# Recurrent matmuls of an LSTM split by gate, and two convolution chunks moved into the projection

## The chip, the core and the metric

The kernel runs on one core of a Trainium2 chip. The metric is the device time of one execution in microseconds (us). Three runs of the kernel before took 1895.57, 1897.46 and 1898.66 us; the median is 1897.46 us. About 0.2% (3.8 us) is what such a measurement can tell from no change.

## What is computed

Two layers, each added to its input. `x` has 8 sequences of 512 steps and 512 features, `cond` one vector of 512 features for each sequence.

```python
# layer 0: LSTM over the 512 steps, h0 = cond, c0 = 0
a = x_t @ Wx + b + h @ Wh              # 8 x 2048: gates i, f, o, g, 512 columns each
c = sigmoid(f) * c + sigmoid(i) * tanh(g)
h = sigmoid(o) * tanh(c)
x = x + h                              # for every step
# layer 1: convolution, projections, scan
# (cond is taken as the 8 taps, one for each of 8 steps)
conv = cb + sum(x_pad[:, k:k + L] * cond[k] for k in range(8))
proj = conv @ Wp + bp                  # 512 -> 128
B_t, C_t = softplus(proj[..., :64]), tanh(proj[..., 64:])
u = x @ Ws + bs
state = decay * state + dt * B_t * u;  y = C_t * state
x = x + y @ Wo + bo
```

## The kernel before

The LSTM is a chain of 512 steps, each of which needs the h of the one before. All instructions of the loop are issued in an order written out by hand; each engine works through its own queue in that order and waits on semaphores.

**Matmuls of a step.** h is held as the stationary operand (`stat`, two buffers that alternate by step): four chunks k of 128 rows, 16 columns of float16 (8 sequences, a high and a low part); in odd steps 32 columns are loaded, of which 16 belong to the step. The weights stream as the moving operand, in two float16 parts, high (`whh`) and low (`whl`). The array is used as four column tiles q of 32, so four matmuls with the same k and part form a group that runs side by side and fills 4 x 32 partitions. The gates of the hidden chunks 0 and 1 form half A, those of chunks 2 and 3 half B. Each half has 256 columns of weights: 64 for each of g, i, f and o. `h_mm` (L308) issues 8 matmuls for one half and one k; the order of (half, k) is `PE_ORDER` (L25). Chunks k = 0, 1 of h come from half A of the step before, k = 2, 3 from half B, so the matmuls with k = 2 or 3 can only start when half B is done too. After the 64 matmuls of h come `bias_mm` (L293) and `x_mm` (L299) of a later step: a bias group and eight groups that multiply x with Wx, 36 matmuls of 256 columns. They start the sum of a pair of steps in the PSUM tile `hp`, which has a bank of its own for each half, twice; half A is started in even steps, half B in odd ones.

**The gates of a step.** The class `Chain` (L549) has one method for each operation, and `ORDER` (L23) names them one after the other, the letter first, then the half: `TA` is T of half A. T (L569) transposes the 192 columns of g, i, f from PSUM on VectorE, t (L572) the 64 columns of o; a (L576, VectorE) and b (L581, GpSimd) add the high and the low part; g (L585) and o (L588) are the tanh on ScalarE, with the sigmoids written as tanh and the weights scaled to suit; v (L591) and c (L595) form the new cell state on VectorE; k (L598) is its tanh and p (L601) its copy into the next step's tile, both on ScalarE; i (L604), m (L607) and l (L610) form h, its high part into `stat`, its full value into `hb`, and its low part into `stat`. Operation l of half A releases the next step's first matmul.

**Layer 1 as filler.** Layer 1 is cut into 14 blocks of 32 steps, one more of 32, and ones of 16, 8 and 8. The work of a block is queued in the class `Filler` (L34) once its steps are through, and is popped a little in each step: one float32 matmul behind the x matmuls (`pl`, `pl2`), VectorE operations at `f` in ORDER up to a planned sum of FILL = 0.8 us (`dve`, `d2`, `xd`), two ScalarE operations at `E`. From step 480 on up to three planned units of matmuls are popped in each step. What is left after the last step is drained at the end. A float32 matmul of 128 x 256 shows as two records in the trace. Their outputs go to the tiles `fps` (two banks); a chain of matmuls holds its bank until it has been read.

The convolution of a block can go two ways for each chunk of 128 features. With the chunk in `pk`, its 8 taps are folded into 8 copies of Wp (`wpj`), and 8 matmuls (L497) do convolution and projection at once. Otherwise one ScalarE operation (L485) and seven VectorE operations (L480) form the convolution, and one matmul projects it (L498). pk is the third number of a row of `l1blocks` (L97): before, it is 0 for all blocks of 32 steps and 4, 4, 2 for the last three.

**PSUM.** Eight banks: four for `hp`, two for `zp` (the sums after a), two for `fps`.

Of the kernel before, what the change touches and what calls it, by code (L numbers as in the profile page):

```python
# [9 lines left out]
F32 = mybir.dt.float32  # L10
# [7 lines left out]
BLK = 32  # L18
NT = BLK * NB
EXP1 = float(1 << 23)  # L20
FMAX = 65504.0

ORDER = "TA tA aA gA bA TB vA oA aB gB cA tB kA pA bB oB vB iA mA cB lA kB pB iB mB lB f q E"  # L23

PE_ORDER = ((0, 0), (0, 1), (1, 0), (0, 2), (0, 3), (1, 1), (1, 2), (1, 3))  # L25
DUMMY = 4
FILL = 0.8
TAILD = 14
LN2 = 0.6931471805599453

# [60 lines left out]
def lstm_conv_ssm_kernel(ctx: ExitStack, tc: tile.TileContext, xT, condT, wx, wh, brow, cbp, wpp, bpp,  # L91
                         wsp, bsp, alogp, dtlogp, wop, bop, outT):
    nc = tc.nc
    T = xT.shape[2]
    NBLK = T // BLK

    l1blocks = [(i * BLK, BLK, 0) for i in range(NBLK - 2)]  # L97
    l1blocks += [(T - 64, 32, 0), (T - 32, 16, 4), (T - 16, 8, 4), (T - 8, 8, 2)]
    v, s, pe, sp = nc.vector, nc.scalar, nc.tensor, nc.sync

    cp = ctx.enter_context(tc.tile_pool(name="cp", bufs=1))
    st = ctx.enter_context(tc.tile_pool(name="st", bufs=2))
    pp = ctx.enter_context(tc.tile_pool(name="pp", bufs=1, space=PSUM))
# [3 lines left out]
    wb = [[cp.tile([128, 4, 4, 512], F16, name=f"w{m}{p}") for p in "hl"] for m in "hx"]  # L107
# [26 lines left out]

    seen = cp.tile([128, 1], F32, name="seen")
    v.memset(seen, 0.0)
    s.activation(seen, seen, AF.Tanh)

    seq = [(0, 0), (1, 0), (1, 1), (1, 2), (1, 3), (0, 1), (0, 2), (0, 3)]
# [20 lines left out]
    gate = [[cp.tile([128, 128], F32, name=f"gate{h}{i}") for i in range(4)] for h in range(2)]  # L160
    x2b = [cp.tile([128, 4, 7 * NB + NT], F32, name=f"x2b{i}") for i in range(3)]

    hpb = [[pp.tile([128, 512], F32, name=f"hp{h}{i}") for i in range(2)] for h in range(2)]
    hp = [[t[:, 0:256] for t in r] for r in hpb]

    zp = [pp.tile([128, 64], F32, name=f"zp{i}") for i in range(2)]
    fps = [pp.tile([128, 2 * NT], F32, name=f"fps{i}") for i in range(2)]

    pool = nc.gpsimd
    ident = cp.tile([128, 128], F32, name="ident")  # L170
# [116 lines left out]

    def warm(n, w):
        for _ in range(n):
            pe.matmul(fps[1][:, 0:256], ident, w, start=True, stop=True)  # L290


    def bias_mm(P, h):  # L293

        for q in range(4):
            pe.matmul(hp[h][P % 2][32 * q:32 * q + 32, :], bst[P > 0][:, q], bmov[:, 256 * h:256 * h + 256],  # L296
                      start=True, stop=False, tile_position=(0, 32 * q), skip_group_check=True)

    def x_mm(P, h, ks):  # L299
        S = xs[P // (BLK // 2) % 2]  # L300
        for k in ks:
            for W in wb[1]:
                for q in range(4):
                    pe.matmul(hp[h][P % 2][32 * q:32 * q + 32, :], S[:, k, P % (BLK // 2)],  # L304
                              W[:, k, q, 256 * h:256 * h + 256],
                              start=False, stop=False, tile_position=(0, 32 * q), skip_group_check=True)

    def h_mm(t, h, ks):  # L308
        S = stat[t % 2]
        o = 16 * (t % 2)  # L310
        for k in ks:
            for wi, W in enumerate(wb[0]):
                for q in range(4):
                    pe.matmul(hp[h][(t // 2) % 2][32 * q:32 * q + o + 16, :], S[:, k, 0:o + 16],  # L314
                              W[:, k, q, 256 * h:256 * h + 256],
                              start=False, stop=(k == 3 and wi == 1),
                              tile_position=(0, 32 * q), skip_group_check=True)


    v.tensor_scalar(bmov[0:64], braw, 1.0 / 2048, None, op0=ALU.mult)  # L320
# [77 lines left out]
    lo(7, 1)  # L398
    for j in range(2):
        v.tensor_scalar(CL[:, j], SW[:, :, 0], FMAX * (1 - 2 * j), None, op0=ALU.mult)  # L400
    for h in range(2):
        bias_mm(0, h)
    for c, (m, k) in enumerate(seq):
        for h in range(2):
            x_mm(0, h, (k,)) if m else h_mm(0, h, (k,))

    cv = carve(0, 0, (4, NT))
    e, w, x = (carve(0, 1024 + 256 * i, (NT,), 64) for i in range(3))
# [140 lines left out]
    class Chain:  # L549
# [4 lines left out]
        def __init__(self, t, half):  # L554
            h = half
            self.o = 16 * (t % 2)
            self.S = stat[(t + 1) % 2][:, 2 * h:2 * h + 2, 16 - self.o:32 - self.o]
            self.G, self.Gn = gate[h][t % 4], gate[h][(t + 1) % 4]
            self.P, self.zp = hp[h][(t // 2) % 2], zp[h]
            self.hf = hb[(t // BLK) % 2][:, 2 * h:2 * h + 2, t % BLK, :]  # L560
            self.inv = 1.0 if t else INV0
            self.Z = st.tile([128, 6, 32], F32, tag=f"Z{h}", name=f"Z{t}_{h}")
            self.Zo = st.tile([128, 2, 32], F32, tag=f"Zo{h}", name=f"Zo{t}_{h}", bufs=4)
            self.zo = st.tile([128, 16], F32, tag=f"zo{h}", name=f"zo{t}_{h}", bufs=4)
            self.u = st.tile([128, 2, 16], F32, tag=f"u{h}", name=f"u{t}_{h}")
            self.tc = st.tile([128, 16], F32, tag=f"tc{h}", name=f"tc{t}_{h}", bufs=4)

        def T(self):
            v.transpose(self.Z.rearrange("p g r -> p (g r)"), self.P[:, 0:192])  # L569

        def t(self):
            v.transpose(self.Zo.rearrange("p g r -> p (g r)"), self.P[:, 192:256])  # L572

        def a(self):
            o = self.o
# [35 lines left out]

    def dummy(n):
        for _ in range(n):
            pe.matmul(hpb[0][0][:, 0:256], wb[0][1][:, 0, 0, 0:128], wb[0][0][:, 0, 0, 0:256], start=True, stop=True)

    def r8(a):
        return a.rearrange("p (k b) -> p k b", b=8)
# [2 lines left out]
    for t in range(T):  # L620
        n, r = divmod(t, BLK)
        if r == 0:
            assert all(h["x2"] in fl.done for h, (b0, *_) in zip(hist, l1blocks) if b0 < t - BLK)
            load_x(n + 2)
            if n + 1 < NBLK:
                add_x(n + 1, 0, t)
        if nl1 < len(l1blocks) and l1blocks[nl1][0] + l1blocks[nl1][1] <= t:
            add_l1(nl1, *l1blocks[nl1])
            nl1 += 1
        if t:  # L630
            for h, k in PE_ORDER:
                h_mm(t, h, (k,))

        P = t // 2 + 1
        if 2 * P < T:
            assert P < 6 or all( xlast[2 * P // BLK, k] in fl.done for k in range(4))
            bias_mm(P, t % 2)
            x_mm(P, t % 2, range(4))
        room = (1 if t < T - 32 else 3) if 2 * P < T else 4
        while room > 0:  # L640
            cost = fl.pop("pl2", t) or fl.pop("pl", t)
            room -= cost
            if not cost:
                break
        ch = {"A": Chain(t, 0), "B": Chain(t, 1)}
        for op in ORDER.split():
            if op == "f":
                left = FILL
                while True:
                    got = fl.pop("xd", t, left) or fl.pop("d2", t, left) or fl.pop("dve", t, left)  # L650
                    left -= got
                    if not got:
                        break
            elif op == "q":

                if t % 2:
                    s.activation(seen, ch["B"].tc[:, 0:1], AF.Copy)
            elif op == "E":
                for _ in range(2):
                    fl.pop("xa", t) or fl.pop("al2", t) or fl.pop("al", t)  # L660
                fl.pop("po", t)
            else:
                getattr(ch[op[1]], "o_" if op[0] == "o" else op[0])()
        fl.pop("sp", t)
    dummy(TAILD)
    while nl1 < len(l1blocks):
        add_l1(nl1, *l1blocks[nl1])
# [8 lines left out]
def layout(x, cond, Wx, Wh, b, cb, Wp, bp, Ws, bs, Al, dl, Wo, bo):  # L676


    import numpy as np

    def rows(w):
        w = w.reshape(4, 4, 32, -1)
        return np.ascontiguousarray(w.transpose(0, 2, 1, 3).reshape(128, 4, -1))

    order = [3, 3, 0, 0, 1, 1, 2, 2] * 2
    chunk = [0, 1] * 4 + [2, 3] * 4
    T = x.shape[1]
    gx = rows(Wx).reshape(128, 4, 4, 4, 4, 32)
    gh = rows(Wh).reshape(128, 4, 4, 4, 4, 32)
    gb = b.reshape(4, 4, 4, 32)  # L690
    wx = np.stack([gx[:, :, g, :, k, :] for g, k in zip(order, chunk)], 3).reshape(128, 4, 4, 512)
    wh = np.stack([gh[:, :, g, :, k, :] for g, k in zip(order, chunk)], 3).reshape(128, 4, 4, 512)
    bb = np.zeros((2, 32, 16, 32), np.float32)
    for n, (g, k) in enumerate(zip(order, chunk)):
        bb[:, 4 * (g != 3):4 * (g != 3) + 4, n] = gb[g, :, k, :]
    bb = bb.reshape(64, 512)
    xT = rows(x.transpose(2, 1, 0).reshape(512, T * 8)).reshape(128, 4, T, 8)
    cT = rows(cond.T)
    wo = Wo.reshape(64, 4, 4, 32).transpose(0, 2, 1, 3).reshape(64, 4, 128)
    c1 = lambda a: np.ascontiguousarray(a.reshape(-1, 1))  # L700
    d = dict(xT=xT, condT=cT, wx=wx, wh=wh, brow=bb, cb=rows(cb)[:, :, 0], wp=rows(Wp), bp=c1(bp),
             ws=rows(Ws), bs=c1(bs), alog=c1(Al), dtlog=c1(dl), wo=wo, bo=rows(bo)[:, :, 0])
    return {k: np.ascontiguousarray(a) for k, a in d.items()}
# [30 lines left out]
```

## Time and profile before

| | |
|---|---|
| median of three runs | 1897.46 us |
| profiled execution, its own time | 1898.87 us |
| its span | 1897.1 us |
| first T of step 0 / of step 511 | 40.97 / 1858.47 us |
| behind the first T of step 511 | 38.55 us |
| granted TensorE clock, mean | 0.992 |
| TensorE matmul busy | 1653.8 us (87%) |
| VectorE busy | 1648.8 us (87%) |
| ScalarE / GpSimd busy | 782.2 / 288.2 us |

Read it so: 511 steps lie between the first T of step 0 and that of step 511, 3.557 us each on average. The busy shares are averages over steps that are all alike in the recurrent part and differ in the filler that they hold. A matmul record lasts from its issue to its modelled end, so the records of groups that follow each other overlap: what a group costs is the distance between the starts of two groups.

### The profile page before, as it was taken

Reading aid. Unit: us, or ns where it says so; the run is one execution under the profiler, and the core shown is the slowest. Engines: PE = TensorE matmul, PEld = TensorE weight load, DVE = VectorE, ACT = ScalarE, POOL = GpSimd, SP = SyncE. Lnnn points to the kernel's source line nnn. Section 1 sums busy time; section 2 is a strip of 40 time slices with the busy share of each in tenths; the row PEclk is TensorE's granted clock in tenths of the full one; section 3 lists DMA queues with packets and bytes.
Section 4 is the critical chain, followed back from the end, with each engine's and each line's share of the span. In section 5 each row is a group of like instructions: output and inputs, shape, how many; then the busy total and the mean of one; then the engine's idle time right before and its main releaser. Section 6 shows DMA issues by size and latency. Waiting matters only on the chain.

```text
span 1897.1 us, 119869 instructions
## 1 busy us (share of the span) xinstructions
PE 1653.8 (87%) x51861; PEld 1364.6 (72%) x51861; DVE 1648.8 (87%) x9137; ACT 782.2 (41%) x4684; POOL 288.2 (15%) x1110
## 2 busy tenths in 40 slices
PE   6888898898988889898898988889898898988896
PEld 4777777777777777777777777777776777777786
DVE  8778889898898989889898898989889898898984
ACT  5544344344434444443444434434443344434342
POOL 1211111111111111111111111111111111111110
PEclk9999999999999999999999999999999999999997
DMA  6000000000000000000000000000000000000000
GB/s 237 4 4 15 4 26 4 4 27 4 26 4 4 27 4 26 4 26 4 4 27 4 26 4 5 26 4 27 4 26 4 4 15 4 15 4 15 4 13 15
DMA packets 21428, 33.52 MB, mean 18 GB/s; under 512 B 2592, under 2 KB 19616, under 8 KB 19872
## 3 DMA queue, kind: packets, MB, share of 16 engines
q1 hardware_dynamic: 20656, 25.71, 4.0%
q8 instruction: 405, 6.64, 1.5%
q14 instruction: 127, 1.04, 0.2%
q10 hardware_dynamic: 240, 0.13, 0.0%
HBM read 17.45 MB, written 8.39 MB: 14 GB/s over the span
## 4 chain that ended last, share of the span: by engine, by line
DVE 50%; PE 31%; ACT 11%; POOL 4%; issue 4%; DMA 0%; ACTq 0%; POOLq 0%; DVEq 0%
PE hp L314 20%; DVE Z L569 16%; DVE wraw L480 7%; DVE zp L576 6%; PE hp L304 5%; ACT gate L585 5%; POOL zo L581 4%; DVE stat L610 3%; DVE stat L604 3%; ACT gate L588 3%; PE fps L501 3%; DVE u L591 3%; DVE Zo L572 3%; ACT tc L598 3%; DVE hb L607 2%
## 5 line engine op out<-in xcount | busy, mean ns | idle before, releaser
L314 PE MATMUL hp<-whh,stat 128*16 128x256 f16 (+1 forms) x16384 | 932.8, 274 | 212.8 <-DVE stat L610 208.4
L314 PEld LDWEIGHTS <-stat 128*16 128x16 f16 x32768 | 777.2, 93 | 443.8 <-DVE stat L610 374.2
L314 PE MATMUL hp<-whl,stat 128*16 128x256 f16 (+1 forms) x16384 | 928.9, 273 | 0.2 <-DVE whl L279 0.2
L585 ACT ACTIVATE gate<-zp 128x48 f32<-128x48 f32 x1022 | 216.2, 212 | 906.1 <-DVE zp L576 903.6
L569 DVE STREAM_TRANSPOSE Z<-hp 128x192 f32<-128x192 f32 x1024 | 391.6, 382 | 111.7 <-PE hp L314 98.4
L304 PE MATMUL hp<-wxh,xs 128*32 128x256 f16 x8192 | 481.6, 273 | 5.5 <-DVE xs L354 5.5
L581 POOL TENSOR_TENSOR zo<-Zo 128x16 f32<-128x16 f32 x1024 | 245.1, 239 | 1571.5 <-DVE zp L576 1092.4
L304 PE MATMUL hp<-wxl,xs 128*32 128x256 f16 x8192 | 481.6, 273 | 0.0
L304 PEld LDWEIGHTS <-xs 128*32 128x32 f16 x16384 | 438.9, 97 | 15.4 <-DVE xs L354 5.7
L588 ACT ACTIVATE gate<-zo 128x16 f32<-128x16 f32 x1022 | 220.6, 216 | 158.1 <-POOL zo L581 141.6
L604 DVE SCALAR_TENSOR_TENSOR stat<-gate,tc 128x16 f16<-128x16 f32 x1024 | 179.5, 175 | 69.0 <-ACT tc L598 0.6
L572 DVE STREAM_TRANSPOSE Zo<-hp 128x64 f32<-128x64 f32 x1024 | 229.9, 225 | 0.0
L576 DVE TENSOR_TENSOR zp<-Z 128x48 f32<-128x48 f32 x1024 | 211.2, 206 | 0.0
L610 DVE TENSOR_TENSOR stat<-hb,stat 128x16 f16<-128x16 f32 x1024 | 179.3, 175 | 17.5
L591 DVE SCALAR_TENSOR_TENSOR u<-gate 128x32 f32<-128x32 f32 x1024 | 175.9, 172 | 20.9 <-ACT tc L598 0.2
L480 DVE SCALAR_TENSOR_TENSOR wraw<-x2b,cond,wraw 128x256 f32<-128x256 f32 (+1 forms) x434 | 188.7, 472 | 4.7 <-ACT wraw L483 4.7
L601 ACT ACTIVATE gate<-zp 128x16 f32<-128x16 f32 x1024 | 188.5, 184 | 0.0
L607 DVE SCALAR_TENSOR_TENSOR hb<-gate,tc 128x16 f32<-128x16 f32 x1024 | 186.3, 182 | 0.0
L598 ACT ACTIVATE tc<-zp 128x16 f32<-128x16 f32 x1024 | 185.2, 181 | 0.4 <-DVE zp L595 0.2
L595 DVE SCALAR_TENSOR_TENSOR zp<-u 128x16 f32<-128x16 f32 x1024 | 177.3, 173 | 0.0
L296 PE MATMUL hp<-bmov,bst 128*32 128x256 f16 x2048 | 144.5, 273 | 0.0
L296 PEld LDWEIGHTS <-bst 128*32 128x32 f16 x2048 | 54.7, 97 | 3.2 <-issue 0.3
(121 smaller groups left out, 739.2 us busy)
## 6 DMA issues: line engine op xcount, KB each, us to landing
x<-in_xT_dram SPq DMA_DIRECT2D x15, 512.0 KB, 4.0
out_dram<-wraw SPq DMA_DIRECT2D x15, 512.0 KB, 4.1
wraw<-in_wh_dram SPq DMA_DIRECT2D x4, 1024.0 KB, 13.7
wraw<-in_wx_dram SPq DMA_DIRECT2D x4, 1024.0 KB, 10.9
x<-in_xT_dram SPq DMA_DIRECT2D x2, 256.0 KB, 12.9
wp<-in_wp_dram SPq DMA_DIRECT2D x1, 256.0 KB, 7.1
out_dram<-wraw SPq DMA_DIRECT2D x1, 256.0 KB, 2.8
out_dram<-wraw SPq DMA_DIRECT2D x2, 128.0 KB, 2.2
```

The source lines that it names most:

```text
L304: pe.matmul(hp[h][P % 2][32 * q:32 * q + 32, :], S[:, k, P % (BLK // 2)], W[:, k, q, 256 * h:256 * h + 256], start=False, stop=False, tile ...
L314: pe.matmul(hp[h][(t // 2) % 2][32 * q:32 * q + o + 16, :], S[:, k, 0:o + 16], W[:, k, q, 256 * h:256 * h + 256], start=False, stop=(k == ...
L480: v.scalar_tensor_tensor(cv[:, k, 0:N], src, cond[:, k, j:j + 1], cv[:, k, 0:N], op0=ALU.mult, op1=ALU.add)
L569: v.transpose(self.Z.rearrange("p g r -> p (g r)"), self.P[:, 0:192])
L572: v.transpose(self.Zo.rearrange("p g r -> p (g r)"), self.P[:, 192:256])
L576: v.tensor_tensor(self.zp[:, 0:48].rearrange("p (g b) -> p g b", b=8), self.Z[:, :, o:o + 8], self.Z[:, :, o + 8:o + 16], op=ALU.add)
L581: pool.tensor_tensor(self.zo.rearrange("p (g b) -> p g b", b=8), self.Zo[:, :, o:o + 8], self.Zo[:, :, o + 8:o + 16], op=ALU.add)
L585: s.activation(self.G[:, 0:48], self.zp[:, 0:48], AF.Tanh, scale=self.inv)
L588: s.activation(self.G[:, 48:64], self.zo, AF.Tanh, scale=self.inv)
L598: s.activation(self.tc, self.zp[:, 48:64], AF.Tanh, scale=0.5)
L604: v.scalar_tensor_tensor(self.S[:, :, 0:8], r8(self.G[:, 48:64]), 1.0, r8(self.tc), op0=ALU.add, op1=ALU.mult)
L610: v.tensor_tensor(self.S[:, :, 8:16], self.hf, self.S[:, :, 0:8], op=ALU.subtract)
```

## The change

- **The columns of the weights are put in another order** (`layout`): half A's g, i, f (192 columns, called A), half B's o (64, called b), half B's g, i, f (192, called B), half A's o (64, called a).
- **The h matmuls are issued in two parts.** The first, ahead of the gates, has the groups A and B, 16 groups of four matmuls with 192 columns each. The second, at `H` in ORDER behind TB, has a and b, 16 groups with 64 columns each. So 128 matmuls take the place of 64.
- **The outputs.** A's sums and b's share a bank of `hpb[0]`, B's have `hpb[1]`, and a's have one new bank `hpo`, without a second buffer. One bank of `fps` is given up for it.
- **The x matmuls** stand at `X` in ORDER, behind tB: in even steps a bias group and eight groups of 256 columns (A and b together), in odd steps the same number of 192 (B) and again of 64 (a).
- **ORDER is new**: t of half A comes behind TB, g of half B ahead of o of half A, vB and cB ahead of iA, pA behind mA.
- **r and R** are new small copies, in each step and in each odd step: on VectorE one column of the cell state that ScalarE wrote, on VectorE and GpSimd one column each, in odd steps.
- **PK = 2**: in all blocks of 32 steps the chunks 0 and 1 of the convolution go through `wpj`. For a block that takes 2 ScalarE and 14 VectorE operations of 256 columns away, and puts 16 float32 matmuls in the place of 2.
- The three banks `hpb[0][0]`, `hpb[0][1]` and `hpb[1][1]` are given to the filler's matmuls after the last step.

In the order of the changed program, 367 steps have one filler matmul of TensorE behind them, 24 have two to four, and 121 none; before it was 170, 18 and 324. Two VectorE fillers stand in 268 steps, before in 377. After the last step 78 float32 matmuls are left, before 73.

```diff
-ORDER = "TA tA aA gA bA TB vA oA aB gB cA tB kA pA bB oB vB iA mA cB lA kB pB iB mB lB f q E"
-PE_ORDER = ((0, 0), (0, 1), (1, 0), (0, 2), (0, 3), (1, 1), (1, 2), (1, 3))
+ORDER = "TA r aA gA TB H tA bA aB vA tB X cA gB bB oA vB cB kA iA mA pA oB lA kB iB pB mB lB f q R E"
+PE_ORDER = ("A0h A0l A1h A1l B0h A2h A2l A3h A3l B0l B1h B1l B2h B2l B3h B3l",
+            "a0h a0l a1h a1l a2h a2l a3h a3l b0h b0l b1h b1l b2h b2l b3h b3l")
+COLS = {"A": (0, 192), "b": (192, 256), "B": (256, 448), "a": (448, 512)}
+PK = 2
...
-    l1blocks = [(i * BLK, BLK, 0) for i in range(NBLK - 2)]
-    l1blocks += [(T - 64, 32, 0), (T - 32, 16, 4), (T - 16, 8, 4), (T - 8, 8, 2)]
+    l1blocks = [(i * BLK, BLK, PK) for i in range(NBLK - 2)]
+    l1blocks += [(T - 64, 32, PK), (T - 32, 16, 4), (T - 16, 8, 4), (T - 8, 8, 2)]
...
-    hp = [[t[:, 0:256] for t in r] for r in hpb]
+    hpo = pp.tile([128, 512], F32, name="hpo")
-    fps = [pp.tile([128, 2 * NT], F32, name=f"fps{i}") for i in range(2)]
+    fps = [pp.tile([128, 2 * NT], F32, name="fps0")]
+    def sums(c, P):
+        if c == "a":
+            return hpo[:, 0:64]
+        return hpb[c == "B"][P % 2][:, slice(192, 256) if c == "b" else slice(0, 192)]
...
+    XG = ("Ab", "B", "a")
+    def group(P, g):
+        if g == "Ab":
+            return hpb[0][P % 2][:, 0:256], slice(0, 256)
+        return sums(g, P), slice(*COLS[g])
...
-    def h_mm(t, h, ks):
+    def h_mm(t, seq):
         S = stat[t % 2]
         o = 16 * (t % 2)
-        for k in ks:
-            for wi, W in enumerate(wb[0]):
-                for q in range(4):
-                    pe.matmul(hp[h][(t // 2) % 2][32 * q:32 * q + o + 16, :], S[:, k, 0:o + 16],
-                              W[:, k, q, 256 * h:256 * h + 256], ...)
+        for c, k, p in seq.split():
+            d = sums(c, t // 2)
+            for q in range(4):
+                pe.matmul(d[32 * q:32 * q + o + 16, :], S[:, int(k), 0:o + 16],
+                          wb[0]["hl".index(p)][:, int(k), q, slice(*COLS[c])], ...)
...
         if t:
-            for h, k in PE_ORDER:
-                h_mm(t, h, (k,))
-        P = t // 2 + 1
-        if 2 * P < T:
-            bias_mm(P, t % 2)
-            x_mm(P, t % 2, range(4))
+            h_mm(t, PE_ORDER[0])
...
+            if op == "H":
+                if t:
+                    h_mm(t, PE_ORDER[1])
+            elif op == "X":
+                P = t // 2 + 1
+                if 2 * P < T:
+                    for g in XG[1:] if t % 2 else XG[:1]:
+                        bias_mm(P, g)
+                        x_mm(P, g, range(4))
...
+            elif op == "r":
+                if t:
+                    v.tensor_copy(seenv[:, 0:1], ch["B"].G[:, 64:65])
+            elif op == "R":
+                if t % 2:
+                    v.tensor_copy(seenv[:, 1:2], ch["B"].zo[:, 0:1])
+                    pool.tensor_copy(seenp, ch["B"].G[:, 48:49])
...
-    chunk = [0, 1] * 4 + [2, 3] * 4
+    chunk = [0, 1] * 3 + [2, 3] * 4 + [0, 1]
```

More of the change, by code (lines that the diff above doesn't have):

```diff
@@ L136, in lstm_conv_ssm_kernel @@
     v.memset(seen, 0.0)
+    seenv, seenp = cp.tile([128, 2], F32, name="seenv"), cp.tile([128, 1], F32, name="seenp")
     s.activation(seen, seen, AF.Tanh)
@@ L289, in warm, with bias_mm, x_mm @@
         for _ in range(n):
-            pe.matmul(fps[1][:, 0:256], ident, w, start=True, stop=True)
-    def bias_mm(P, h):
+            pe.matmul(hpb[1][1][:, 0:256], ident, w, start=True, stop=True)
+    XG = ("Ab", "B", "a")
[3 more added lines that the diff above has]
+        return sums(g, P), slice(*COLS[g])
+    def bias_mm(P, g):
+        d, c = group(P, g)
         for q in range(4):
-            pe.matmul(hp[h][P % 2][32 * q:32 * q + 32, :], bst[P > 0][:, q], bmov[:, 256 * h:256 * h + 256],
+            pe.matmul(d[32 * q:32 * q + 32, :], bst[P > 0][:, q], bmov[:, c],
                       start=True, stop=False, tile_position=(0, 32 * q), skip_group_check=True)
-    def x_mm(P, h, ks):
+    def x_mm(P, g, ks):
         S = xs[P // (BLK // 2) % 2]
+        d, c = group(P, g)
         for k in ks:
@@ L303, in x_mm @@
                 for q in range(4):
-                    pe.matmul(hp[h][P % 2][32 * q:32 * q + 32, :], S[:, k, P % (BLK // 2)],
-                              W[:, k, q, 256 * h:256 * h + 256],
+                    pe.matmul(d[32 * q:32 * q + 32, :], S[:, k, P % (BLK // 2)], W[:, k, q, c],
                               start=False, stop=False, tile_position=(0, 32 * q), skip_group_check=True)
-    def h_mm(t, h, ks):
+    def h_mm(t, seq):
         S = stat[t % 2]
         o = 16 * (t % 2)
-        for k in ks:
-            for wi, W in enumerate(wb[0]):
-                for q in range(4):
[L314 to L317, printed above, removed]
+        for c, k, p in seq.split():
+            d = sums(c, t // 2)
+            for q in range(4):
+                pe.matmul(d[32 * q:32 * q + o + 16, :], S[:, int(k), 0:o + 16],
+                          wb[0]["hl".index(p)][:, int(k), q, slice(*COLS[c])],
+                          start=False, stop=k + p == "3l", tile_position=(0, 32 * q), skip_group_check=True)
     v.tensor_scalar(bmov[0:64], braw, 1.0 / 2048, None, op0=ALU.mult)
@@ L400, in lstm_conv_ssm_kernel @@
         v.tensor_scalar(CL[:, j], SW[:, :, 0], FMAX * (1 - 2 * j), None, op0=ALU.mult)
[L401 to L405, printed above, removed]
+    for g in XG:
+        bias_mm(0, g)
+    for m, k in seq:
+        if m:
+            for g in XG:
+                x_mm(0, g, (k,))
+        else:
+            h_mm(0, " ".join(f"{c}{k}{p}" for c in "ABab" for p in "hl"))
     cv = carve(0, 0, (4, NT))
@@ L558, in __init__ @@
             self.G, self.Gn = gate[h][t % 4], gate[h][(t + 1) % 4]
-            self.P, self.zp = hp[h][(t // 2) % 2], zp[h]
+            self.P, self.Po = sums("AB"[h], t // 2), sums("ab"[h], t // 2)
+            self.zp = zp[h]
             self.hf = hb[(t // BLK) % 2][:, 2 * h:2 * h + 2, t % BLK, :]
@@ L568, in T @@
         def T(self):
-            v.transpose(self.Z.rearrange("p g r -> p (g r)"), self.P[:, 0:192])
+            v.transpose(self.Z.rearrange("p g r -> p (g r)"), self.P)
         def t(self):
-            v.transpose(self.Zo.rearrange("p g r -> p (g r)"), self.P[:, 192:256])
+            v.transpose(self.Zo.rearrange("p g r -> p (g r)"), self.Po)
         def a(self):
@@ L613, in dummy @@
         for _ in range(n):
-            pe.matmul(hpb[0][0][:, 0:256], wb[0][1][:, 0, 0, 0:128], wb[0][0][:, 0, 0, 0:256], start=True, stop=True)
+            pe.matmul(hpb[1][0][:, 0:256], wb[0][1][:, 0, 0, 0:128], wb[0][0][:, 0, 0, 0:256], start=True, stop=True)
     def r8(a):
@@ L630, in lstm_conv_ssm_kernel @@
         if t:
-            for h, k in PE_ORDER:
-                h_mm(t, h, (k,))
-        P = t // 2 + 1
-        if 2 * P < T:
-            assert P < 6 or all( xlast[2 * P // BLK, k] in fl.done for k in range(4))
-            bias_mm(P, t % 2)
-            x_mm(P, t % 2, range(4))
[L639 to L644, printed above, removed]
+            h_mm(t, PE_ORDER[0])
         ch = {"A": Chain(t, 0), "B": Chain(t, 1)}
         for op in ORDER.split():
-            if op == "f":
+            if op == "H":
[4 more added lines that the diff above has]
+                if 2 * P < T:
+                    assert P < 6 or all(xlast[2 * P // BLK, k] in fl.done for k in range(4))
+                    for g in XG[1:] if t % 2 else XG[:1]:
+                        bias_mm(P, g)
+                        x_mm(P, g, range(4))
+                room = (1 if t < T - 32 else 3) if 2 * P < T else 4
+                while room > 0:
+                    cost = fl.pop("pl2", t) or fl.pop("pl", t)
+                    room -= cost
+                    if not cost:
+                        break
+            elif op == "f":
                 left = FILL
@@ L664, in lstm_conv_ssm_kernel @@
         fl.pop("sp", t)
+    for b in (hpb[0][0], hpb[0][1], hpb[1][1]):
+        fl.free[len(fl.banks)] = -10
+        fl.banks.append(b)
     dummy(TAILD)
```

## The prediction

> **What bounds the kernel now.** I read four views in this order: the page's chain and costliest groups, the timeline of a step with a float32 filler matmul, that of one without, and that of one of the late steps that hold two.
>
> ```profile
> DVE 50%; PE 31%; ACT 11%; POOL 4%; issue 4%; DMA 0%; ACTq 0%; POOLq 0%; DVEq 0%
> ...
> L314 PEld LDWEIGHTS <-stat 128*16 128x16 f16 x32768 | 777.2, 93 | 443.8 <-DVE stat L610 374.2
> ...
> L569 DVE STREAM_TRANSPOSE Z<-hp 128x192 f32<-128x192 f32 x1024 | 391.6, 382 | 111.7 <-PE hp L314 98.4
> ```
>
> TensorE waits for VectorE's last product of h (L610), VectorE for the sums of TensorE (L314): a ring that goes round once a step. ScalarE and GpSimd lie inside it, DMA nowhere.
>
> ```profile
> 902.02 0.70 PE L501 MATMUL fps<-wraw,wp 128*128 128x256 f32 x2
> ...
> 902.50 0.18 DVE L610 TENSOR_TENSOR stat<-hb,stat 128x16 f16<-128x16 f32 x1
> ...
> 902.73 1.65 PEld L314 LDWEIGHTS <-stat 128*32 128x32 f16 x64 [0.41 <-DVE stat L610]
> ...
> 904.06 0.38 DVE L569 STREAM_TRANSPOSE Z<-hp 128x192 f32<-128x192 f32 x1
> ...
> 904.71 0.38 DVE L569 STREAM_TRANSPOSE Z<-hp 128x192 f32<-128x192 f32 x1
> ```
>
> h starts at 902.73, 0.05 us after half A's L610 ended. TA starts at 904.06, 1.33 us later; the next h starts at 906.27, 2.21 us after TA. Together 3.54.
>
> ```profile
> 923.07 0.28 PE L304 MATMUL hp<-wxl,xs 128*32 128x256 f16 x4
> 923.99 0.29 PE L314 MATMUL hp<-whh,stat 128*32 128x256 f16 x4 [0.64 <-DVE stat L610]
> ```
>
> Without a filler matmul the last x group still lies 0.92 us before the next h, and the step is just as long: over the run, steps with none, with one and with VectorE fillers all take 3.54 to 3.55 us. The fillers are hidden, but hardly:
>
> ```profile
> 1757.23 0.28 PE L304 MATMUL hp<-wxl,xs 128*32 128x256 f16 x4
> 1757.45 1.08 PE L492 MATMUL fps<-x2b,ws 128*64 128x256 f32 x4
> 1758.45 0.29 PE L314 MATMUL hp<-whh,stat 128*16 128x256 f16 x4
> ```
>
> With two fillers (four records) h comes at 1758.45, 0.08 us ahead of the modelled end of the last one (1757.45 + 1.08), and the step takes 3.84 us. That is what TensorE-bound looks like. So with one filler of 0.70 us, h could start 0.22 + 0.70 - 0.08 = 0.83 us after the last x group's start, against some 0.91 as it is: **0.08 us of slack**, in every step that holds one.
>
> **Cost of a group.** Groups of 256 columns start 0.1092 us apart (902.85 to 904.38 is 14 groups). The two records of a float32 matmul, which streams its 256 columns twice in each, end 0.216 us apart in the trace. Taking 512c + f = 0.216 and 256c + f = 0.1092 gives 0.417 ns per column and f = 2.4 ns per group. By this estimate 192 columns cost 0.0825 us, **64 columns 0.029 us**. No row shows so short a group. Its bounds: 0.027 us, if all of the 0.1092 scales with the columns, and 0.109 us, if nothing does because eight instructions set it. I take 0.029: the trace has the four loads and four matmuls of a group issue within 12 ns, and the second group's loads follow the first's after 15 ns, so 256 columns, not the issue, set the distance. TensorE's queue could still run dry when it needs an instruction every 3.6 ns for 128 in a row; the steady rate seen is one in 13.6 ns.
>
> The Trainium skill speaks against this part. "TensorEngine Tiling (Array Packing)", section Instruction Overhead, gives each matmul some 60 cycles however few its columns, and warns against tiling a dimension that is small already. The issue rows above show that four matmuls do not pay one after the other; if they did, the page's figure would make 0.1 us of a short group, and the sum below some 550 us worse.
>
> **Steps with a filler matmul (367 with one).** All of TensorE's work stands in line: 16 groups of 192 columns, 1.32; 16 of 64, 0.467; x in even steps 9 x 0.1092 = 0.983, in odd steps 9 x (0.0825 + 0.029) = 1.005; from there to the next h 0.83 - 0.109 = 0.72; the first group's delay 0.01. Even 3.50, odd 3.525, mean **3.513**, where the step was 3.547: -0.034 each, **-12.5 us**. TensorE's own sum was 16 x 0.1092 + 0.983 + 0.72 + 0.01 = 3.46; it grows by 2.4 ns for each of 16 (odd: 25) more groups, while the ring gets shorter than it (next part): these steps turn TensorE-bound. Both switches between column tiles and the whole array around a filler are in the 0.83.
>
> **Steps without one (121).** TA needs the ninth group, not the tenth: 0.01 + 8 x 0.0825 + 0.25 (a 192-column matmul's life: 0.28 - 0.027) + 0.06 = 0.98 us after h starts instead of 1.33: -0.35. TB follows 7 groups later, 0.58 after TA, when aA has gone. Then tA and aB stand ahead of vA on VectorE: tA 0.88, aB 1.01, vA 1.13 after TA (it was 0.96); cA 1.37 (1.19), kA 1.59 (1.43), iA 1.81 (1.67), lA 2.11 (1.98) and h at 2.33 (2.21): +0.12. So the move of the o columns costs a third of what it brings; r fits between T and aA, which start 0.43 apart with 0.30 taken (a copy, L529, holds VectorE for 0.09). The ring is 3.31, -0.23. a is ready 8 short groups behind B, 0.2 us before tA, and b in time for tB; at 0.109 us each a would hold tA, and all of VectorE behind it, by 0.6. Half B's h is ready 0.40 after half A's, just as the five groups that don't need it (0.42) are through. The new wait of b's first group for TA ends 0.2 us before that group's turn; that of a's x group in odd steps for tA, 0.4 before.
>
> The o gate of A: GpSimd starts b 0.14 after t ends (its first row comes that long after L572 in the timeline), so bA at 1.23, oA at 1.49 to 1.70, 0.1 before iA needs it.
>
> With two VectorE fillers TA comes later: lB at 2.50, 0.09 to the first, 0.396 + 0.405 for both (distances of such starts in the trace): 3.39 in even, some 3.5 with R ahead of TA in odd steps. 29 of the 121 lie in the first 33 steps, nearly bare: 29 x 0.23 = **-6.6 us**. Of the other 92, two thirds hold two (mean 3.46): 3.42, -0.125 each, **-11.5 us**.
>
> **Fillers moved.** 15 blocks x 14 VectorE operations x 0.478 us = 100 us leave VectorE, and 15 x 14 matmuls x 0.43 us = 90 us of streaming come to TensorE. Both kinds were hidden; VectorE's fillers still are, except in some 60 steps without a matmul. TensorE's are not: a filled step is 0.2 longer than the bare ring, which is why only a quarter of the steps gain much. With one `fps` bank chains queue up, but the program's order keeps pace.
>
> **The end.** From step 480 on two to three fillers stand in most steps and TensorE bound many of them before too (3.70 to 3.90): 2.4 ns for some 20 more groups in each of 32 steps, +1. Behind the last step 5 more matmuls (5 x 0.43) and some 4 VectorE operations (4 x 0.48): between 0 and +4; I take **+3**. The start-up has 16 groups more at step 0: below 1.
>
> **Sum.** -12.5 - 6.6 - 11.5 + 1 + 3 = -26.6. The profiled execution took 1898.87 (its span 1897.1 and 1.8 around it); against it 1872.3, and by the median of the runs, 1.4 lower, **1871 us**, -1.4%. Its own range is 1860 to 1890.
>
> **Rivals.**
> 1. *Slower: the short groups cost more than their columns.* Place: the 64-column groups of h and x in the 391 filled steps, 16 in even and 24 in odd ones, 7,820 in all; each ns beyond 29 costs 7.8 us. It decides from 29 + 26.6/7.8 = 32.4 ns. At 36 ns 1925 us, at 40 ns 1956, at the upper bound of 109 ns 2500 and more. For it: 2.8 times the instruction rate, an instruction fetch of 16 KB that took 1.1 us and would be due every 2.5 instead of 4.5 us, the mean load record of 93 ns. Against it: the close issue, and loads that a background buffer takes in while the group before streams. Chance 0.30 slower, 0.07 within 0.2%.
> 2. *TensorE does not bind the filled steps* (the next h slips under the float32 matmul's end): then all steps follow the ring, about 3.42 on average: 511 x 0.127 = 65 us less, 4 given back at the end, 1836. For it: nothing in before waits at one filler. Against it: the late steps' 1758.45. Chance 0.05.
> 3. *Leaving a short group costs as much as leaving a long one*: 0.22 us between last x group's start and filler in odd steps also after 64 columns, +0.08 in 195 steps: +16, 1887. The trace has only the drain after 256 columns. Chance 0.07.
>
> My forecast has 0.51. Below 1893.7 us is faster, above 1901.3 slower (0.2%, about what a measurement of this kernel can tell from no change): faster 0.51 + 0.05 + 0.07 = 0.63, same 0.07, slower 0.30. The range from 1858 to 1925 leaves out rival 2 and rival 1 beyond 36 ns, together below 0.2.
>
> **What would show it.** Groups of `hpo` start 0.029 apart and VectorE's t never waits for TensorE; the wait of L314's loads for L610 shrinks to nearly nothing in filled steps, which last 3.50 to 3.53, and bare ones last 3.3; VectorE's busy time hardly changes (-100 us of taps, 767 copies of at most 0.163, L529's row). I am wrong if hpo's groups lie 0.033 or more apart, if a bare step stays above 3.45, or if filled steps match bare ones.

## The result

| | before | after |
|---|---|---|
| median of the runs | 1897.35 us (1895.57 to 1898.66) | 2802.39 us (2800.14 to 2816.76) |
| profiled span | 1897.1 us | 2800.7 us |
| first T of step 0 / of step 511 | 40.97 / 1858.47 us | 41.04 / 2757.34 us |
| mean step | 3.557 us | 5.316 us |
| granted TensorE clock | 0.992 | 0.973 |

The changed kernel takes **1.479 times** the time (95% interval 1.474 to 1.484): 905 us more. Nearly all of it lies in the steps, 511 x 1.759 = 899 us. The granted clock differs by 2%, far too little for this.

Of the page of the changed kernel, in its order: the engines' busy time, the queue that fetches instructions, the chain that ended last by engine, and three of the costliest groups (busy us, mean ns of one | idle time of the engine just before them, and what ended most of it).

```profile
PE 2017.0 (72%) x94265; PEld 1678.7 (60%) x94265; DVE 1638.3 (58%) x9694; ACT 763.9 (27%) x4654; POOL 316.4 (11%) x1366
...
q8 instruction: 736, 12.06, 1.8%
...
PE 68%; issue 27%; DVE 5%; ACT 0%; POOL 0%; DVEq 0%; POOLq 0%
...
L336 PEld LDWEIGHTS <-stat 128*16 128x16 f16 x65536 | 1030.8, 94 | 633.9 <-issue 513.5
...
L594 DVE STREAM_TRANSPOSE Z<-hp 128x192 f32<-128x192 f32 x1024 | 391.9, 383 | 863.0 <-PE hp L336 861.5
...
L336 PE MATMUL hpo<-whl,stat 128*16 128x64 f16 (+1 forms) x8192 | 241.8, 195 | 41.2 <-issue 40.9
```

VectorE was half of the chain and is 5% of it; "issue", which was 4%, is 27%. Before, the loads of h waited 374.2 us for the L610 of VectorE; now 513.5 us for "issue", which is time in which the engine waits for nothing that the profile shows. VectorE has hardly less to do (1638.3 us, 1648.8 before), but T now waits 861.5 us for TensorE's sums (98.4 before). So TensorE sets the pace, and it is busy for only 72% of the span. The views of the waits and of the timeline say where the rest goes. The waits of the changed kernel (us in total, times, longest):

```profile
DVE Z L594 <- PE hp L336: 861.5, 605, 4.5
PEld L336 <- issue: 513.5, 634, 3.2
PEld L327 <- issue: 349.5, 191, 3.2
PE hp L336 <- issue: 302.0, 350, 3.0
...
DVE Zo L597 <- PE hp L336: 98.8, 107, 2.2
DVE Zo L597 <- PE hpo L336: 80.9, 103, 2.1
...
PEld L336 <- DVE stat L635: 55.2, 141, 0.6
```

The wait for h that closed the ring of the kernel before (L635 is its L610) has shrunk to 55 us, as it should. "Issue" has taken its place, at the loads and matmuls of h (L336) and of x (L327) alike. TensorE's timeline of the changed kernel (start, duration, line, tiles, count [idle before <- releaser]):

```profile
1290.98 0.29 PE L327 MATMUL hp<-wxl,xs 128*32 128x256 f16 x3
1292.72 0.27 PE L327 MATMUL hp<-wxl,xs 128*32 128x256 f16 x1 [1.45 <-issue]
...
1300.08 0.20 PE L336 MATMUL hpo<-whh,stat 128*16 128x64 f16 x3
1300.11 0.20 PE L336 MATMUL hpo<-whl,stat 128*16 128x64 f16 x3
1300.14 0.21 PE L336 MATMUL hpo<-whh,stat 128*16 128x64 f16 x4
1300.17 0.21 PE L336 MATMUL hpo<-whl,stat 128*16 128x64 f16 x4
...
1302.50 0.25 PE L336 MATMUL hp<-whl,stat 128*32 128x192 f16 x1
1303.41 0.26 PE L336 MATMUL hp<-whl,stat 128*32 128x192 f16 x3 [0.66 <-issue]
```

The 64-column groups do start 0.03 us apart. But at 1290.98 three matmuls of a group of four go out and the fourth 1.7 us later, and at 1302.50 one goes out and its three neighbours 0.9 us later. These share a stationary chunk, a part of the weights and a bank; no data can be missing for one that is there for the other. Such a stop falls elsewhere each time, in groups of x as of h, of 256 columns as of 192.

What they have in common is their place in the instruction stream. I numbered TensorE's records in order (loads and matmuls; the trace has one for each instruction) and took every stretch of more than 0.3 us between two starts, from 100 to 2700 us (in the kernel before, to its end):

| | stretches, us in all | at one position in 256 | most at any other position |
|---|---|---|---|
| changed kernel | 1000.7 | 850.2 (648 stretches) | 3.9 |
| kernel before | 367.2 | no such position | 6.2 |

All 412 stretches over 1 us of the changed kernel stand at that position. It lies where one block of 256 instructions of 64 bytes, a packet of 16,384 bytes of the instruction queue, gives way to the next. Before, TensorE has 103,722 loads and matmuls, 405 blocks; after, 188,530, 736 blocks: just the queue's packets. The queue's row (packets, MB, share) on the page of the kernel before:

```profile
q8 instruction: 405, 6.64, 1.5%
```

After, the row above says 736. In the trace a packet takes some 1.0 us, and the next starts 3.71 us after it (median; 3.24 the shortest). Before, the median was 4.29 and the shortest 3.44. 736 x 3.71 = 2731 us: **TensorE waits for its instructions.**

The starts of the packets and of TensorE's records show it one by one. In the changed kernel the first instruction at that position starts 1.2 to 1.6 us after the packet before has ended (5% to 95%; median 1.4), and the next packet starts 1.1 us after that instruction (median; up to 1.7). In the kernel before, the same instruction comes 2.1 to 3.9 us after the packet: the block is there well before it is needed.

The Trainium skill says otherwise: "Runtime: NRT & Kernel Launch", section Instruction fetch mechanics, has the fetch in 16 KiB blocks as seen here, but "The cost of crossing a 16 KiB boundary is one DMA tail-bump, mostly hidden." Here 850 us of stops stand at the crossing, and the measurement decides.

### The profile page after: what moved, and what is told of

The parts are those of the page before. It is cut to its first block, busy times and chain, and to the rows that moved or that the text cites. A ratio compares the mean times of both kernels' runs of the same rounds, so it can differ in the third digit from the quotient of the medians.

```text
span 2800.7 us, 204424 instructions
## 1 busy us (share of the span) xinstructions
PE 2017.0 (72%) x94265; PEld 1678.7 (60%) x94265; DVE 1638.3 (58%) x9694; ACT 763.9 (27%) x4654; POOL 316.4 (11%) x1366
## 4 chain that ended last, share of the span: by engine, by line
PE 68%; issue 27%; DVE 5%; ACT 0%; POOL 0%; DVEq 0%; POOLq 0%
PE hp L336 35%; PE hp L327 13%; PE fps L525 7%; PE hpo L336 6%; PE hpo L327 3%; PE hp L318 2%; PE fps L516 1%; PE fps L560 1%; DVE Zo L597 1%; DVE zp L620 1%; DVE stat L635 1%; DVE u L616 0%; DVE wxl L292 0%; DVE whl L292 0%; PE hp L560 0%
## 5 line engine op out<-in xcount | busy, mean ns | idle before, releaser
L336 PEld LDWEIGHTS <-stat 128*16 128x16 f16 x65536 | 1030.8, 94 | 633.9 <-issue 513.5
L336 PE MATMUL hp<-whh,stat 128*16 128x192 f16 (+2 forms) x24576 | 1037.8, 234 | 176.9 <-issue 158.0
L336 PE MATMUL hp<-whl,stat 128*16 128x192 f16 (+2 forms) x24576 | 1040.3, 234 | 144.6 <-issue 144.1
L594 DVE STREAM_TRANSPOSE Z<-hp 128x192 f32<-128x192 f32 x1024 | 391.9, 383 | 863.0 <-PE hp L336 861.5
L610 ACT ACTIVATE gate<-zp 128x48 f32<-128x48 f32 x1022 | 214.9, 210 | 1848.9 <-DVE zp L601 1848.7
L327 PEld LDWEIGHTS <-xs 128*32 128x32 f16 x24576 | 498.9, 97 | 357.1 <-issue 349.5
L327 PE MATMUL hp<-wxl,xs 128*32 128x256 f16 (+1 forms) x8192 | 472.2, 262 | 108.4 <-issue 108.4
L327 PE MATMUL hp<-wxh,xs 128*32 128x256 f16 (+1 forms) x8192 | 471.6, 262 | 93.2 <-issue 87.5
L336 PE MATMUL hpo<-whl,stat 128*16 128x64 f16 (+1 forms) x8192 | 241.8, 195 | 41.2 <-issue 40.9
L336 PE MATMUL hpo<-whh,stat 128*16 128x64 f16 (+1 forms) x8192 | 236.7, 196 | 35.4 <-issue 34.6
L635 DVE TENSOR_TENSOR stat<-hb,stat 128x16 f16<-128x16 f32 x1024 | 190.7, 186 | 35.0
L525 PE MATMUL fps<-x2b,wraw 128*128 128x256 f32 (+2 forms) x576 | 185.3, 417 | 4.2 <-issue 4.2
L597 DVE STREAM_TRANSPOSE Zo<-hp 128x64 f32<-128x64 f32 x512 | 125.0, 244 | 99.1 <-PE hp L336 98.8
L318 PE MATMUL hp<-bmov,bst 128*32 128x256 f16 (+1 forms) x2048 | 154.7, 269 | 27.3 <-issue 27.3
```

Of the source, the lines that this page charges most:

```text
L318: pe.matmul(d[32 * q:32 * q + 32, :], bst[P > 0][:, q], bmov[:, c], start=True, stop=False, tile_position=(0, 32 * q), skip_group_check=True)
L327: pe.matmul(d[32 * q:32 * q + 32, :], S[:, k, P % (BLK // 2)], W[:, k, q, c], start=False, stop=False, tile_position=(0, 32 * q), skip_gro ...
L336: pe.matmul(d[32 * q:32 * q + o + 16, :], S[:, int(k), 0:o + 16], wb[0]["hl".index(p)][:, int(k), q, slice(*COLS[c])], start=False, stop=k ...
L525: pe.matmul(bk["b"][:, 0:N], w_, r_, start=m == 0, stop=m == len(mms) - 1)
L594: v.transpose(self.Z.rearrange("p g r -> p (g r)"), self.P)
L610: s.activation(self.G[:, 0:48], self.zp[:, 0:48], AF.Tanh, scale=self.inv)
```

## Experiments

Theory I is this supply: a block of 256 every 3.7 us. With the 67 us by which the changed kernel's span of 2800.7 us exceeds its 736 x 3.715, it gives a time for any number of blocks, where the supply sets the pace. The rivals are that the short groups cost what they look like costing (S), that the moved convolution does (P), and that loads are dear in themselves (L). The first, second and fourth experiment are one execution each; their differences are in the hundreds of us.

**Fewer loads, same matmuls.** A pass over the finished program leaves out a weight load when the same tile of the array still holds that operand (and no semaphore hangs on the load):

```diff
+def once(nc):
+    for block in nc.main_func.blocks:
+        held, keep = {}, []
+        for i in block.instructions:
+            op = str(i.opcode)
+            if op == "Ldweights":
+                key, what = str(i.tile_position), (str(i.ins), str(i.tile_size))
+                sync = i.sync_info
+                if held.get(key) == what and not (sync and (sync.on_wait or sync.on_update)):
+                    continue
+                held[key] = what
+            elif op == "Matmult" and i.ldweights is not False:
+                held = {}
+            keep.append(i)
+        block.instructions = keep
```

> The changed kernel with every weight load left out that loads what the tile still holds: the same 93,732 matmuls, in the same order and with the same 64-column groups, but 50,085 loads in place of 93,198 (145,419 TensorE instructions in 568 blocks of 256, where the changed kernel has 188,532 in 736). Theory I (TensorE is short of instructions: a block of 256 every 3.715 us, the median between two fetches in the changed kernel): 568 x 3.715 + 67 us outside = 2177 us, and still fetch after fetch. Rival S (the short groups and the extra matmuls themselves cost the time): about as the changed kernel, 2750 to 2800 us, since every matmul is still there.

Measured: 2204.13 us. With each short group still there, 598 us are gone, for 168 blocks fewer: 3.56 us a block. S is out. Its page:

```profile
q8 instruction: 568, 9.31, 1.8%
...
PE 79%; issue 12%; DVE 8%; ACT 0%; DMA 0%; ACTq 0%; DVEq 0%
```

The chain still has 12% of "issue", fetches follow at 3.74 us (median), and of 479.3 us of stretches over 0.3 us (from 100 us after the start to 100 us before the end) 325.8 stand at the same position in 256: the supply still binds. The clock was 0.991 here, 0.992 in the kernel before, so the clock is not the reason for the stops.

**The split alone.**

```diff
-PK = 2
+PK = 0
```

> The changed kernel with the taps of all chunks back on VectorE as before (PK 0): the split alone. Theory I: 733 blocks in place of 736, so 733 x 3.715 + 67 = 2790 us, and VectorE's added work lies in TensorE's idle time. Rival P (the 14 more float32 matmuls a block of layer 1, each of four instructions and a stop between the tiles, cost it): near the kernel before, 1900 us.

Measured: 2816.23 us, where the changed kernel's own runs reach from 2800 to 2817. P is out as the cause. Of 1123.7 us of stretches over 0.3 us, 976.8 stand at the one position in 256.

**The moved convolution alone.**

```diff
-    l1blocks = [(i * BLK, BLK, 0) for i in range(NBLK - 2)]
-    l1blocks += [(T - 64, 32, 0), (T - 32, 16, 4), (T - 16, 8, 4), (T - 8, 8, 2)]
+    l1blocks = [(i * BLK, BLK, 2) for i in range(NBLK - 2)]
+    l1blocks += [(T - 64, 32, 2), (T - 32, 16, 4), (T - 16, 8, 4), (T - 8, 8, 2)]
```

> The kernel before with the change's second part alone: two chunks' taps in Wp for all blocks, no split. Theory I: 408 blocks in place of 405, and 1897 us hold 501 at 3.715 us, so supply does not bind: 1870 to 1910 us. Rival P: clearly slower, hundreds of us.

Measured: 1912.91 us, 1.0063 times the kernel before (1.0046 to 1.0080), a little over the expected range. So this part costs some 14 us there: 6.6 in the steps (3.570 us each on average, 3.557 before) and 7.4 behind them (46.0 us after the last first T, 38.55 before).

**Extra instructions in the kernel before.** No group is split here; 12 groups that stream next to nothing are added to each step.

```diff
+    zero = cp.tile([128, 16], F16, name="zero")
+    pool.memset(zero, 0.0)
...
+    def dose(P, h, n):
+        S = xs[P // (BLK // 2) % 2]
+        for _ in range(n):
+            for q in range(4):
+                pe.matmul(hp[h][P % 2][32 * q:32 * q + 32, 0:16], S[:, 0, P % (BLK // 2)], zero,
+                          start=False, stop=False, tile_position=(0, 32 * q), skip_group_check=True)
...
             x_mm(P, t % 2, range(4))
+            dose(P, t % 2, 12)
```

> The kernel before with 12 groups of four matmuls by 16 zero columns added to each step's x work (into sums that they do not change): 96 TensorE instructions a step, 596 blocks in all, and 12 x 16 columns at 2.4 columns per ns = 0.08 us of array time a step. Theory I: 596 x 3.715 + 67 = 2281 us, fetch after fetch, though no group of the kernel before is split. Rival S (the added array time and the groups' own cost, 0.08 to 0.36 us a step by groups 0.007 to 0.03 us apart, in the filled steps where TensorE binds): 1930 to 2080 us.

Measured: 2299.34 us, 400 us more than the kernel before (1899.22 beside it) and far above what S allows. Its timeline:

```profile
1002.23 0.30 PE L314 MATMUL hp<-zero,xs 128*32 128x16 f16 x23
1003.21 0.33 PE L314 MATMUL hp<-zero,xs 128*32 128x16 f16 x25 [0.67 <-issue]
1003.38 0.29 PE L323 MATMUL hp<-whh,stat 128*16 128x256 f16 x4
```

Once the instructions are there, 25 zero matmuls with their loads take 0.17 us, 3.4 ns an instruction, so these instructions themselves need little time. In the middle of the 48 stands a stop of 0.67 us. Of 541.3 us of stretches over 0.3 us 439.5 stand at the one position in 256, the same as in the changed kernel.

**A quarter of the dose, and loads left out of the kernel before.** The first has `dose(P, t % 2, 3)`, the second the pass `once` on the kernel before.

> The kernel before with 3 groups of four matmuls by 16 zero columns a step, in place of the 12 of the fourth experiment: 24 TensorE instructions a step, 453 blocks. Theory I: 453 x 3.745 + 67 = 1764 us of supply, under 1897, so there is slack and only the array time counts, 3 x 0.007 to 3 x 0.03 us in the steps that TensorE binds (367): 1900 to 1930 us. Rival S (a price per instruction or group, the same at each dose): a quarter of the 400 us that 12 groups cost, 1999 us.

> The kernel before with every weight load left out that loads what the tile still holds: 79,099 TensorE instructions in 309 blocks, where it has 405. Theory I: the kernel before, at 202 instructions a step against 242 that 3.745 us a block would allow in its 3.547 us, is not bound by the supply, so 1885 to 1900 us. Rival L (each weight load costs TensorE time of its own, 94 ns in the records, and the removed loads of the first experiment gained for that reason and not for the supply): 24,600 loads fewer, in groups of four, would give back up to 6,150 x 0.094 = 580 us at the far end, and in any case much over 1%.

Measured: 1901.11 us for the small dose, 1.0008 times the kernel before (0.9997 to 1.0019): 24 instructions a step cost nothing, 96 cost 400 us. A price per instruction is out; there is a threshold, as a supply has one. Without the repeated loads 1893.18 us, 0.9970 (0.9959 to 0.9981): 24,600 loads fewer are worth 6.2 us, so L is out too; and in the changed kernel the short groups start 0.030 us apart with all loads and 0.029 without the repeated ones. In neither run does one position in 256 hold more than 5 us of stretches. Two pages; of the small dose:

```profile
q8 instruction: 453, 7.42, 1.6%
...
DVE 46%; PE 35%; ACT 11%; POOL 4%; issue 3%; DMA 0%; ACTq 0%; POOLq 0%; DVEq 0%
```

and of the kernel before without the repeated loads:

```profile
q8 instruction: 309, 5.06, 1.1%
...
DVE 49%; PE 31%; ACT 11%; POOL 4%; issue 4%; DMA 1%; SPq 1%; POOLq 0%; DVEq 0%; ACTq 0%
```

From 309 to 453 blocks the chain keeps its shape, "issue" at 3 to 4%.

**The split with few instructions.** If the supply is the cause, the split itself need not cost anything. The o columns of both halves become one group of 128 columns, read from the old column layout by a strided view, in one bank; x for o stands with B's; layer 1's matmuls come in even steps, where no x for o is; PK is 0 and the pass `once` is on.

```diff
+PE_ORDER = ("A0h A0l A1h A1l B0h B0l A2h A2l A3h A3l B1h B1l B2h B2l B3h B3l",
+            "o3h o3l o2h o2l o1h o1l o0h o0l")
+COLS = {"A": 0, "B": 256}
+ROOM = (1, 0)
+PK = 0
...
+    def sums(c, P):
+        if c == "o":
+            return hpo[:, 0:128]
+        return hpb[c == "B"][P % 2][:, 0:192]
+    def cols(a, c):
+        if c == "o":
+            return a.rearrange("p (h c) -> p h c", c=256)[:, :, 192:256]
+        return a[:, COLS[c]:COLS[c] + 192]
...
+                    for c in "Bo" if t % 2 else "A":
+                        bias_mm(P, c)
+                        x_mm(P, " ".join(f"{c}{k}{p}" for k in range(4) for p in "hl"))
+                room = (ROOM[t % 2] if t < T - 32 else 3) if 2 * P < T else 4
```

> The split with few instructions. The o columns of both halves are one group of 128 columns in one bank of their own (a strided view of the weights, in the column layout of the kernel before), the x work of o stands with half B's in odd steps, layer 1's matmuls are popped in even steps, PK is 0, and loads of what a tile still holds are left out: 115,931 TensorE instructions, 453 blocks (736 in the changed kernel, 405 before). Same columns through the array as before. Theory I: 453 blocks hold 1764 us, so supply does not bind and the split pays what the dependences allow: the filled step (TensorE full) at 3.46 in place of 3.547 us, 1855 to 1880 us. Rival S (the split itself, o's matmuls after the others and their transposes later, is what costs): 2000 us or more.

Measured: 1881.58 us, **0.9904 times the kernel before (0.9887 to 0.9920)**, faster than both kernels; 1.6 us outside the expected range. Its page:

```profile
PE 1710.5 (91%) x77461; PEld 1063.7 (57%) x38468; DVE 1683.4 (90%) x9904; ACT 776.1 (41%) x4684; POOL 319.6 (17%) x1366
...
q8 instruction: 453, 7.42, 1.6%
...
DVE 78%; PE 15%; issue 3%; ACT 3%; DMA 0%; ACTq 0%; DVEq 0%
```

The mean step is 3.508 us (3.557 before), 25 us in all, of which 8.6 are given back behind the last step (47.2 us where it was 38.55). The chain now runs on VectorE.

All kernels beside the theory's sum, in the order of their blocks; the interval is that between the starts of two fetches:

| kernel | blocks | interval, 5% / median / 95% (us) | blocks x 3.715 + 67 | measured |
|---|---|---|---|---|
| before, fewer loads | 309 | 4.53 / 6.33 / 6.90 | 1215 | 1893 |
| before | 405 | 3.71 / 4.29 / 5.80 | 1572 | 1897 |
| before, PK 2 | 408 | 3.55 / 4.29 / 5.78 | 1583 | 1913 |
| before, 3 groups more | 453 | 3.48 / 4.00 / 5.06 | 1750 | 1901 |
| split, one group for o | 453 | 3.44 / 3.82 / 4.81 | 1750 | 1882 |
| after, fewer loads | 568 | 3.38 / 3.74 / 4.29 | 2177 | 2204 |
| before, 12 groups more | 596 | 3.38 / 3.73 / 4.32 | 2281 | 2299 |
| after, PK 0 | 733 | 3.39 / 3.72 / 4.34 | 2790 | 2816 |
| after | 736 | 3.37 / 3.71 / 4.08 | 2801 (fitted) | 2802 |

Where the sum is above 1900 us, the time follows it to 1.3%, and the median interval is 3.71 to 3.74 us, whatever the matmuls are. Where it is below, other work sets the time, and the intervals stretch to fit. The three of these that were not fitted came out 18 to 27 us over the sum; their intervals are a little longer (mean 3.74 to 3.75 us against 3.71 in the changed kernel), and why was not tried.

## Why the prediction was wrong

**The step that failed** is the end of "Cost of a group": "TensorE's queue could still run dry when it needs an instruction every 3.6 ns for 128 in a row; the steady rate seen is one in 13.6 ns", after which the short group was taken at 0.029 us and the supply at nothing. A filled step of the changed kernel issues 368 TensorE instructions, 204 before: 368 / 256 x 3.71 = 5.33 us of supply, where 3.513 was predicted. Its median is 5.23.

**Rival 1** had the sign, and even the evidence: a fetch that takes 1.1 us and would be due every 2.5 us. I read the 1.1 us as the period that the queue can keep, so 2.5 seemed ample. But 1.1 us is one packet, and the next does not follow at once: the trace of before, which is in no hurry in many steps, shows no two fetches closer than 3.44 us. That minimum was there to be read, and 736 x 3.44 = 2532 us would have been the estimate. The rival's price was wrong as well: to reach 2802 us its short groups would have to cost 29 + 931 / 7.82 = 148 ns each, over its own upper bound of 109. And two of its figures were off: the "2.8 times the instruction rate" is 1.8 by the prediction's own steps (368 in 3.513 us against 204 in 3.547), and the odd steps have 25 short groups, as its part on filled steps has it, not 24.

**What a short group costs** was nearly right. In the changed kernel eight groups of a start from 1300.08 to 1300.29, 0.030 us apart, and those of b, by the same view, from 1300.38 to 1300.61, 0.033; without the repeated loads it is 0.029. 1 to 4 ns on 7,820 groups are 8 to 31 us, which would have mattered in a forecast of -26 and is little beside 905. The section Instruction Overhead of the Trainium skill's "TensorEngine Tiling (Array Packing)", with some 60 cycles for each matmul, is not borne out as a price that four matmuls pay one after the other: four of them share 0.03 us. A least price for the group there may be: in the small dose, by the starts of its matmuls, groups of 16 columns follow each other after 0.0265 us, hardly less than those of 64.

**Filled and bare steps.** I had named "filled steps match bare ones" as a sign of error, and they nearly do: 5.23 and 5.09 us (medians). Neither 3.513 nor 3.31 could show itself under the supply. The split with one group for o gives the parts of the bare step a trial, in another layout and without the repeated loads (which alone took 0.012 us off the mean step of the kernel before). Of its timeline:

```profile
1001.56 0.27 PE L332 MATMUL hp<-whh,stat 128*32 128x192 f16 x4
...
1002.61 0.38 DVE L586 STREAM_TRANSPOSE Z<-hp 128x192 f32<-128x192 f32 x1
...
1005.05 0.26 PE L332 MATMUL hp<-whh,stat 128*16 128x192 f16 x4 [0.15 <-DVE stat L627]
```

T of half A starts 1.05 us after the first h matmul, 1.33 before. By the prediction's terms it would be 1.06, since T needs ten groups there and not nine: so the gain from letting T start after 192 columns is real. The way back costs more than forecast: from T to the next h the median is 2.35 to 2.43 us by kind of step, where 2.33 was predicted and 2.22 measured before. Among the first 470 steps, the 67 that hold neither a filler matmul nor a VectorE filler take 3.46 (even) and 3.47 us (odd), above the 3.45 that the prediction named as a sign of error; -0.23 is not confirmed, and how much of that the other layout does was not tried. Steps with a filler matmul, all of them even, take 3.41 us, those without 3.53 (medians, steps 20 to 470), and the mean step is 0.049 us shorter than before.

**"t never waits for TensorE"** fell with the rest: t waits 80.9 us for a and 98.8 for b. **Fillers moved**: hidden in the changed kernel, in TensorE's idle time (without the move it takes 2816.23 us, no less); but in the kernel before the same move alone costs 6.6 us in the steps, which I had at nothing. **The end**: +4.8 us behind the last first T (43.3 against 38.55), where I had +3 and 4 as the bound. **Rivals 2 and 3** could not show under the supply. Two small slips change nothing in this: 2.4 ns for 20 groups in 32 steps are 1.5 us, not 1, and at 0.109 us each the groups of a would hold tA by some 0.4 us, not 0.6, as a has 0.2 in hand.

## What to carry to other kernels

Count the instructions of each engine as well as its columns: on this chip TensorE got 256 instructions in 3.7 us, one in 14.5 ns, so by this estimate an average of more than some 245 in a step of 3.55 us sets the pace whatever the array has to do. In the runs some 226 a step (3 groups more) cost nothing and 284 (the changed kernel with fewer loads) set the pace; between them lies no run. How near a kernel stands to that is seen in its own trace, from the instruction queue's packets and the shortest distance between two of them (3.2 to 3.4 us in all runs but one, somewhat less than the 3.7 that the queue kept up), not from how long one takes. Splitting a matmul doubles its loads too; a load of what the tile still holds can be left out, and columns that lie apart can go through as one strided group.

## What the runs showed of the hardware

- **TensorE's instruction queue kept up one block of 16 KB every 3.7 us** where it set the pace (median; 5% to 95% 3.4 to 4.3), though a packet takes only 1.0 to 1.1 us. In the four kernels that it held back, the block's first instruction starts 1.4 us after the packet's end and the next packet 1.1 us after that instruction (medians). Why these two take so long no run here shows.
- **The stop stands at one instruction in 256**, and inside a block instructions go out at 3.4 ns each, so a single burst may be faster than the supply; 24 instructions more in each step cost nothing while the average stayed below it.
- **A weight load that repeats the last one can be left out**: the matmuls go on with what the tile holds. Where the supply binds, 43,100 loads were worth 598 us; where it doesn't, 24,600 were worth 6.
